# A Mamba layer on one core: the directions' B and C rows side by side in DRAM, the middle group's partitions taken in turn, the prologue's pieces spread, and the last states entering through the first token

## The chip, the cores and the metric

The kernel runs on one NeuronCore of one Trainium2 chip. The metric is the device time of one execution in microseconds, from the first to the last instruction. The kernel before takes 13002.14 us (median of three runs, 12996.56 to 13002.71); the execution that the profile shows has a span of 13002.5 us. All times below are from that profiled execution.

## The reference, cut to what matters

Two images of 96 channels and 128 x 128 pixels go through two layers. The first layer mixes with a selective scan (Mamba) in four directions and then has a quantised feed-forward part; the second mixes with a 3 x 3 convolution and has the same kind of feed-forward part. The change lies in the scan of the first layer alone. For each of the four directions, over the L = 16384 tokens of an image, with 192 inner channels d and 16 states s:

```
xc, z = split(x @ in_w.T);  u = silu(causal_conv4(xc) + conv_b)
dt_raw, B, C = split(u @ xproj_w.T)            # 6, 16, 16 columns
dt = softplus(dt_raw @ dt_w.T + dt_b);  A = -exp(A_log)
for every token t:                             # state h has 192 x 16 values
    h = exp(dt_t[:, None] * A) * h + dt_t[:, None] * B_t[None, :] * u_t[:, None]
    y_t = (h * C_t[None, :]).sum(over s)
out = ((y + Dp * u) * silu(z)) @ outp_w.T
```

B_t and C_t depend on the token and the state, not on the channel: each of their rows has to reach every partition that holds a channel.

## The kernel before, in words

The four directions are two pairs: rows with their columns forwards, and both backwards (PAIRS). The two directions of a pair have 2 x 192 = 384 channels together, that is three groups g of 128 partitions. Group 0 is all of the first direction, group 2 all of the second; the middle group 1 holds the last 64 channels of the first direction on partitions 0 to 63 and the first 64 of the second on partitions 64 to 127.

An image's scan runs over 64 *steps*: (pair, i) with 32 tiles of T = 512 tokens per pair. A step has 24 *units* (g, s): one group and two of its 16 states. The function mamba writes the instructions of all engines in a fixed order by hand (in_order), in one loop over k; I call one turn of it a *slot*, numbered 0 to 23 within a step. In the slot of unit k stand

- on ScalarE (ACT): the decays exp(dt * A) of unit k+2, two activations into a PSUM tile da (decay, L330; three such tiles), and a copy of the last token's state of unit k-1 into hst (L410);
- on GpSimd (POOL): b_part of unit k+2 (L324), which multiplies the fetched B rows by dt * u;
- on VectorE (DVE): two scans (L334) of 512 tokens, one per state, and between them the product of unit k-1's states with the C rows (L409). A scan starts from the column of hst that the step before left, or from the constant 0.0 in the first tile of a pair;
- on TensorE (PE): two identity matmuls that add unit k-1's products into one PSUM tile y per group (sums, L341). The first unit of a group opens y with the skip term (L416), and there is one such tile (ps_y has one buffer).

When a group is finished, gated (DVE, L349) multiplies y by silu(z). That happens in the slot after the next group's first unit: slots 9 (group 0), 17 (group 1) and slot 1 of the next step (group 2). Only then can the next y be opened. I use these three instants to cut a step into thirds: A from slot 1 to slot 9, B from slot 9 to slot 17, C from slot 17 to slot 1 of the next step.

In between lie the pieces that prepare the *next* step (prologue): conv and gate (PE, L207) with their evacuations conv_out and gate_out (ACT, L233, L241), two silu activations with a table load on each side (ACT, L244), the rows matmul and its evacuation rows_out (L251, L258), and for every group the softplus: dt_in (PE), dt_exp and dt_ln (three activations each), and dt_q, dt_log, dt_sum, dt_u (four tensor operations on POOL). A list of (slot, 0 or 1, piece) says where each is issued: 0 ahead of the slot's hst copy and decays, 1 behind them. The project and collect of the finished groups sit in slots 19 and 3. All PE pieces but the sums share one PSUM tile (misc, one buffer), so a conv waits until the piece before it was evacuated.

The B and C rows go through DRAM: rows_out writes four copies of 64 rows (bcd), and row_tile reads them back, four states of 512 tokens to every partition (8 KB each), 1 MB per tile. For groups 0 and 2 that is one DMA over 128 partitions, for group 1 two DMAs over 64. A tile serves two units; B tiles have four buffers, C tiles three. All DMAs are issued by SyncE (SP) in program order, and each waits there until its buffer is free.

Of the kernel before, what the change touches and what calls it, by code (L numbers as in the profile page):

```python
# [10 lines left out]
F32 = mybir.dt.float32  # L11
# [4 lines left out]
ALU = mybir.AluOpType  # L16
# [4 lines left out]
C = 96  # L21
# [11 lines left out]
COPIES = 4  # L33
# [9 lines left out]
def tile_metaformer(ctx: ExitStack, tc: tile.TileContext, a: dict, out: bass.AP):  # L43
# [35 lines left out]
    nc.vector.memset(gmat, 0.0)  # L79
    with tc.tile_pool(name="prep", bufs=1) as pp, tc.tile_pool(name="prep_ps", bufs=2, space=PSUM) as pps:  # L80
        alog = pp.tile([128, 2, NG, S], F32, name="alog")
        nc.sync.dma_start(alog, a["alog"])
        nc.scalar.activation(alog, alog, AF.Exp)
        nc.vector.tensor_scalar_mul(amat, alog, -1.0)

        dskip = pp.tile([128, 2, NG], F32, name="dskip")
        nc.sync.dma_start(dskip, a["dskip"])
        for pi in range(2):
            for g in range(NG):
                nc.vector.tensor_scalar_mul(dmat[:, pi, g, :], ident, dskip[:, pi, g : g + 1])  # L90

        inxw = pp.tile([C, 4, DI], F32, name="inxw")
        nc.sync.dma_start(inxw, a["inx"])
        taps = pp.tile([C, 4, 4, DI], F32, name="taps")
        nc.sync.dma_start(taps, a["taps"].broadcast_to((C, 4, 4, DI)))
        for d in range(4):
            nc.vector.tensor_tensor(inx[:, d], taps[:, d], inxw[:, d, None, :].broadcast_to((C, 4, DI)), ALU.mult)
        outw = pp.tile([C, 4, DI], F32, name="outw")
        nc.sync.dma_start(outw, a["outw"])
        fusew = pp.tile([C, 4, C], F32, name="fusew")  # L100
        nc.sync.dma_start(fusew, a["fusew"])
        for pi, (da, db) in enumerate(PAIRS):

            pieces = [
                (slice(0, 128), da, 0, 128),
                (slice(0, 64), da, 128, 192),
                (slice(64, 128), db, 0, 64),
                (slice(0, 128), db, 64, 192),
            ]
            for g, (rows, d, lo, hi) in enumerate(pieces):  # L110
                ps = pps.tile([128, C], F32, name="ps")
                nc.tensor.matmul(ps[rows, :], outw[:, d, lo:hi], fusew[:, d, :], start=True, stop=True)
                nc.vector.tensor_copy(gmat[rows, pi, g, :], ps[rows, :])
# [69 lines left out]
    def mamba(acc, xnr, xnc):  # L183

        with ExitStack() as st:
# [5 lines left out]
            hst = one.tile([128, NG, S], F32, name="hst")  # L191
            acc_w = acc.rearrange("c (h w) -> c w h", w=W)
# [17 lines left out]
            def prologue(pi, i, d):  # L210
# [19 lines left out]
                def conv_out(g):  # L230
                    if g == 0:
                        d["xc"] = two.tile([128, NG, T], F32, name="xc")
                    nc.scalar.activation(d["xc"][:, g, :], d["ps"], AF.Identity, bias=convb[:, pi, g : g + 1])  # L233
# [4 lines left out]
                def gate_out(g):  # L238
                    if g == 0:
                        d["sz"] = two.tile([128, NG, T], F32, name="sz")  # L240
                    nc.scalar.copy(d["sz"][:, g, :], d["ps"])  # L241
# [13 lines left out]
                def rows_out():  # L255

                    d["rows"] = one.tile([BCO + NBC, T], F32, name="rows")
                    nc.scalar.copy(d["rows"], d["ps"][0 : BCO + NBC, :])  # L258
                    d["bcd"] = rows_d.tile([COPIES, 2, NBC // 2, T], F32, name="bcd")
                    for n in range(COPIES):  # L260
                        nc.sync.dma_start(d["bcd"][n].rearrange("k r t -> (k r) t"), d["rows"][BCO:, :])
# [39 lines left out]
                at = [(0, 0, load), (8, 1, partial(silu, "xc")), (14, 1, partial(silu, "sz"))]  # L301
                at += [(12, 0, rows), (12, 1, rows_out)]
                for g, k in enumerate((4, 5, 6)):
                    at += [(k, 0, partial(conv, g)), (k, 1, partial(conv_out, g))]
                for g, k in enumerate((7, 10, 11)):
                    at += [(k, 0, partial(gate, g)), (k, 1, partial(gate_out, g))]
                for g, k in enumerate((13, 18, 21)):
                    pieces = (0, 0, dt_in), (0, 1, dt_exp), (1, 1, dt_ln), (2, 0, dt_q), (3, 0, dt_log), (3, 0, dt_sum), (4, 0, dt_u)
                    at += [(k + m, where, partial(f, g)) for m, where, f in pieces]
                return sorted(at, key=lambda p: p[:2])  # L310

            def row_tile(d, g, s, k, ahead):

                t = gen.tile([128, 4, T], F32, name=f"row{k}", bufs=ahead + 1)
                for half in range(2) if g == 1 else (slice(None),):
                    rows = slice(half * 64, half * 64 + 64) if g == 1 else half
                    at = s + S * (half if g == 1 else g // 2)
                    n = (64 if g == 1 else 128) // COPIES
                    src = d["bcd"][None, :, k, at : at + 4, :].broadcast_to((n, COPIES, 4, T))
                    nc.sync.dma_start(t[rows], src)  # L320
                return t

            def b_part(d, g, b):
                nc.gpsimd.tensor_tensor(b, d["dtu"][g][:, None, :].broadcast_to((128, 2, T)), b, ALU.mult)  # L324

# [7 lines left out]
            def scan(i, g, s, j, da, b, h):  # L333
                nc.vector.tensor_tensor_scan(  # L334
                    h[:, j, :], da[:, j, :], b[:, j, :],
                    0.0 if i == 0 else hst[:, g, s + j : s + j + 1], ALU.mult, ALU.add,
                )
# [53 lines left out]
            def feed(k):  # L391
                if k < total:
                    n = k // nu
                    b_part(state[n], units[k % nu][0], bs[k])
# [41 lines left out]
            for k in range(total + 6):  # L436
                n, u = divmod(k, nu)
                if u == 0 and n + 1 < len(steps):
                    for m, where, f in prologue(*steps[n + 1], state[n + 1]):
                        later(k + m, where, f)  # L440
                if k % 2 == 0:
                    fetch(k + 2 * B_AHEAD, 0, B_AHEAD, bs)
                feed(k + AHEAD)
                issue(k, 0)
                if k < total:
                    (_, i), (g, s) = steps[n], units[u]
                    da, b = das.pop(k), bs.pop(k)
                    hs[k] = b if (g, s) in BY_POOL else da
                    scan(i, g, s, 0, da, b, hs[k])
                if 0 < k <= total:  # L450
                    behind(k - 1)
                if k < total:
                    scan(i, g, s, 1, da, b, hs[k])
# [112 lines left out]
def _layout(v):  # L566
# [3 lines left out]
    rows = lambda w: w[order].reshape(2, NG, 128, -1).transpose(2, 0, 1, 3)  # L570
# [3 lines left out]
    for pi, pair in enumerate(PAIRS):  # L574
        for k, d in enumerate(pair):
            at = slice(k * DI, (k + 1) * DI)
            for j in range(2):
                to = slice(BCO + (2 * j + k) * S, BCO + (2 * j + k + 1) * S)
                bcw[pi, at, to] = xw[d, RK + j * S : RK + (j + 1) * S].T
            bcw[pi, at, k * RK : (k + 1) * RK] = xw[d, :RK].T  # L580
            dtw[k * RK : (k + 1) * RK, pi, at] = v["L0_conv_dt_w"][d].T
    grouped = lambda w: w.reshape(2, NG, 128, -1).transpose(2, 0, 1, 3)
# [6 lines left out]
        "convb": rows(v["L0_conv_conv_b"])[..., 0],  # L589
        "bcw": grouped(bcw),  # L590
        "dtw": dtw,
# [3 lines left out]
        "outw": v["L0_conv_outp_w"].transpose(1, 0, 2),  # L595
# [27 lines left out]
```

## Time and profile before

| engine | busy in the whole span, us | share |
|---|---|---|
| VectorE (DVE) | 11569.1 | 89% |
| TensorE (PE) matmuls | 10850.3 | 83% |
| GpSimd (POOL) | 9215.4 | 71% |
| ScalarE (ACT) | 8560.0 | 66% |
| DMA engines | mean of sixteen | 83.1% (queue 1) |

The busy share is an average. The scans of one image take about 5770 us; in their slices DVE and the DMA engines show nine tenths or more, POOL seven to eight, ACT six, PE eight. Between the two images lie some 720 us, and at the end some 570 us, of the other layers (and the normalisation ahead of the second scan), in which DVE falls to four or five tenths; the change doesn't touch them. Durations in the list of groups are from an instruction's start to its end; neighbours on one engine overlap by about 90 ns, so the distance from start to start is a little shorter than the duration.

### The profile page before, as it was taken

The numbers are of one execution on the slowest core, as the hardware profiler recorded it, in microseconds if no ns is written. First come the engines' busy times: TensorE is split into PE (matmuls) and PEld (weight loads), VectorE is DVE, ScalarE is ACT, GpSimd is POOL, SyncE is SP. The second block draws the span as 40 slices with busy tenths as digits, with TensorE's granted clock in tenths as the row PEclk, the third lists the DMA queues.
The fourth block names the chain that finished last, engine by engine and source line by source line (L and its number), as shares of the span: only waits on it lengthen the run. The fifth ranks groups of instructions, "written<-read, shape, count | busy, mean of one in ns | idle before, by whom it ended". The sixth has DMA issues, their size and how long they took to land. (4 is left out here: it accounts for less than half of the span.)

```text
span 13002.5 us, 97992 instructions
## 1 busy us (share of the span) xinstructions
PE 10850.3 (83%) x24208; PEld 3987.1 (31%) x24208; DVE 11569.1 (89%) x10865; ACT 8560.0 (66%) x14738; POOL 9215.4 (71%) x4772
## 2 busy tenths in 40 slices
PE   6888888888888888888978888888888888888889
PEld 2323233333333333333323333332333333333233
DVE  5999999999999999995459999999999999999954
ACT  6666666666666666665566666666666666666655
POOL 4877778777787787772147778777787777877721
PEclk8999999999999999999989999999999999999999
DMA  7999999999999999992079999999999999999920
GB/s 226 287 294 282 298 288 285 295 283 298 288 285 295 283 295 289 285 295 68 13 226 285 298 283 292 290 285 298 285 291 291 284 298 286 290 294 281 296 61 13
DMA packets 545331, 3400.40 MB, mean 262 GB/s; under 512 B 81612, under 2 KB 82732, under 8 KB 146840
## 3 DMA queue, kind: packets, MB, share of 16 engines
q1 hardware_dynamic: 544760, 3394.12, 83.1%
q8 instruction: 195, 3.19, 0.1%
q14 instruction: 376, 3.08, 0.1%
HBM read 3288.94 MB, written 104.86 MB: 261 GB/s over the span
## 5 line engine op out<-in xcount | busy, mean ns | idle before, releaser
L324 POOL TENSOR_TENSOR row<-dtu,row 128x1024 f32<-128x1024 f32 x3072 | 7175.7, 2358 | 1739.3 <-DMA row<-bcd 1419.2
L334 DVE TENSOR_TENSOR_SCAN da<-da,hst,row 128x512 f32<-128x512 f32 x5952 | 7339.4, 1274 | 351.2 <-ACT da L330 194.6
L341 PE MATMUL y<-row,ident 128*128 128x512 f32 x12288 | 6120.1, 626 | 1113.3 <-DVE row L409 1098.9
L330 ACT ACTIVATE da<-dt,amat 128x512 f32<-128x512 f32 x6144 | 4249.4, 692 | 207.5 <-ACT hst L410 0.4
L341 PEld LDWEIGHTS y<-row,ident 128*128 128x128 f32 x12288 | 2288.9, 197 | 4779.4 <-DVE row L409 2292.3
L409 DVE TENSOR_TENSOR row<-da,row 128x1024 f32<-128x1024 f32 x3072 | 3705.9, 1206 | 19.6 <-DMA row<-bcd 18.8
L410 ACT COPY hst<-da 128x2 f32<-128x2 f32 x3072 | 484.0, 158 | 2235.5 <-DVE row L409 2233.3
L416 PE MATMUL y<-xc,dmat 128*128 128x512 f32 x768 | 526.1, 773 | 779.1 <-DVE sz L349 779.1
L287 POOL TENSOR_TENSOR q<-e,q 128x512 f32<-128x512 f32 x384 | 488.0, 1271 | 821.8 <-ACT hst L410 709.1
L233 ACT ACTIVATE xc<-misc,convb 128x512 f32<-128x512 f32 x384 | 264.2, 688 | 1117.5 <-PE misc L207 1117.5
L207 PE MATMUL misc<-xa,inx 96*128 96x512 f32 (+1 forms) x2048 | 932.4, 597 | 59.0 <-DMA xa<-xnr 57.2
L207 PE MATMUL misc<-xb,inx 96*64 96x512 f32 (+1 forms) x2048 | 928.1, 595 | 1.6 <-ACT xc L233 1.6
L531 POOL TENSOR_TENSOR acc<-acc,y 96x512 f32<-96x512 f32 x128 | 147.6, 1153 | 987.0 <-DVE y L530 987.0
L541 PE MATMUL pc<-pad,kw 96*96 96x512 f32 x1152 | 566.7, 593 | 0.0
L207 PEld LDWEIGHTS misc<-xa,inx 96*128 96x128 f32 (+1 forms) x2048 | 323.6, 163 | 625.5 <-issue 493.4
L293 POOL TENSOR_TENSOR dt<-dt,ln 128x512 f32<-128x512 f32 x384 | 486.9, 1268 | 30.1
L297 POOL TENSOR_TENSOR dtu<-dt,xc 128x512 f32<-128x512 f32 x384 | 488.5, 1272 | 0.5
L290 POOL TENSOR_TENSOR ln<-ln,q 128x512 f32<-128x512 f32 x384 | 488.1, 1271 | 0.5
L359 PE MATMUL misc<-sz,gmat 128*96 128x512 f32 x1024 | 483.6, 594 | 0.0
L416 PEld LDWEIGHTS y<-xc,dmat 128*128 128x128 f32 x768 | 129.0, 211 | 1102.1 <-DVE sz L349 1099.1
L268 PE MATMUL misc<-rows,dtw 12*128 12x512 f32 x768 | 439.7, 652 | 18.5 <-ACT dt L275 17.2
L132 DVE TENSOR_TENSOR xq<-xm,rs 96x512 fp8e5<-96x512 f32 x128 | 87.9, 687 | 387.8 <-ACT rs L128 387.8
(75 smaller groups left out, 8403.8 us busy)
## 6 DMA issues: line engine op xcount, KB each, us to landing
row<-bcd SPq DMA_DIRECT2D x2048, 1024.0 KB, 7.5
row<-bcd SPq DMA_DIRECT2D x2048, 512.0 KB, 8.0
bcd<-rows SPq DMA_DIRECT2D x512, 128.0 KB, 9.8
xa<-xnr SPq DMA_DIRECT2D x124, 193.1 KB, 5.8
xb<-xnc SPq DMA_DIRECT2D x124, 193.1 KB, 5.5
acc<-in_x_dram SPq DMA_DIRECT2D x16, 768.0 KB, 17.8
xnr<-xn SPq DMA_DIRECT2D x16, 768.0 KB, 4.3
xnc<-stg SPq DMA_DIRECT2D x16, 768.0 KB, 5.6
```

The costliest lines, as they stand in the source:

```text
L207: nc.tensor.matmul(ps[rows, :], w(PAIRS[pi][d], k, lo, hi), src[d][:, k : k + T], **se)
L287: nc.gpsimd.tensor_tensor(d["q"], d["e"], d["q"], ALU.subtract)
L290: nc.gpsimd.tensor_tensor(d["ln"], d["ln"], d["q"], ALU.add)
L293: nc.gpsimd.tensor_tensor(d["dt"][g], d["dt"][g], d["ln"], ALU.add)
L297: nc.gpsimd.tensor_tensor(dtu, d["dt"][g], d["xc"][:, g, :], ALU.mult)
L324: nc.gpsimd.tensor_tensor(b, d["dtu"][g][:, None, :].broadcast_to((128, 2, T)), b, ALU.mult)
L330: nc.scalar.activation(da[:, j, :], d["dt"][g], AF.Exp, scale=amat[:, pi, g, s + j : s + j + 1])
L334: nc.vector.tensor_tensor_scan(h[:, j, :], da[:, j, :], b[:, j, :], 0.0 if i == 0 else hst[:, g, s + j : s + j + 1], ALU.mult, ALU.add,)
L341: nc.tensor.matmul(y, ident, c[:, j, :], start=False, stop=s + j == S - 1)
L409: nc.vector.tensor_tensor(c, h, c, ALU.mult)
L416: nc.tensor.matmul(y, dmat[:, pi, g, :], d["xc"][:, g, :], start=True, stop=False)
L541: nc.tensor.matmul(pc, kw[:, t, :], rows, start=t == 0, stop=t == 8)
```

## The change: what it does

There are four edits.

1. *One copy, ordered by use.* bcd has one copy instead of four. Its rows are ordered as [B or C][quarter of the states][direction][4 states], so that for each tile the two directions' 8 KB lie next to each other. A tile is always one DMA over 128 partitions; in group 1 even partitions read the first direction, odd ones the second.
2. *The middle group's partitions in turn.* For that the weights of group 1 are permuted on their way in (perm), so that its partitions alternate between the directions. The convolution and gate matmuls still give the old order (convb stays plain), so group 1's results go into a side tile (mix_xc, mix_sz) and two DMAs each, of 64 partitions with step 2, put them in their places. The output weights (outx) come padded, and the memset of gmat falls away.
3. *Last states through the first token.* Every scan starts from 0.0. For a tile i > 0, entering computes for each group exp(A * dt of the first token) * hst (one activation and one POOL product on 128 x 16), and b_part adds it to the first column of B (one POOL addition on 128 x 2 per unit). The copies into hst stay.
4. *Pieces spread.* The prologue's pieces move to other slots, as the list shows; group 1 comes first in conv and gate.

```
-                at = [(0, 0, load), (8, 1, partial(silu, "xc")), (14, 1, partial(silu, "sz"))]
-                at += [(12, 0, rows), (12, 1, rows_out)]
-                for g, k in enumerate((4, 5, 6)):
-                    at += [(k, 0, partial(conv, g)), (k, 1, partial(conv_out, g))]
-                for g, k in enumerate((7, 10, 11)):
-                    at += [(k, 0, partial(gate, g)), (k, 1, partial(gate_out, g))]
-                for g, k in enumerate((13, 18, 21)):
-                    pieces = (0, 0, dt_in), (0, 1, dt_exp), (1, 1, dt_ln), (2, 0, dt_q), (3, 0, dt_log), (3, 0, dt_sum), (4, 0, dt_u)
+                at = [(0, 0, load), (8, 1, partial(silu, "xc")), (13, 1, partial(silu, "sz"))]
+                at += [(12, 1, rows), (13, 0, rows_out), (13, 1, rows_to_dram)]
+                at += [(5, 0, partial(mix, "xc")), (10, 1, partial(mix, "sz"))]
+                for g, k, where in ((1, 3, 1), (0, 5, 0), (2, 6, 1)):
+                    at += [(k, where, partial(conv, g)), (k + 1, where, partial(conv_out, g))]
+                for g, k in ((1, 9), (0, 10), (2, 11)):
+                    at += [(k, 1, partial(gate, g)), (k + 1, 0, partial(gate_out, g))]
+                for g, k in enumerate((14, 17, 20)):
+                    pieces = (0, 1, dt_in), (1, 0, dt_exp), (1, 1, dt_ln), (3, 0, dt_q), (4, 0, dt_log), (4, 0, dt_sum), (5, 0, dt_u)
...
+                def mix(name):
+
+                    for k in range(2):
+                        nc.sync.dma_start(d[name][k:128:2, 1, :], d["mix", name][64 * k : 64 * k + 64, :])
...
-                    d["bcd"] = rows_d.tile([COPIES, 2, NBC // 2, T], F32, name="bcd")
-                    for n in range(COPIES):
-                        nc.sync.dma_start(d["bcd"][n].rearrange("k r t -> (k r) t"), d["rows"][BCO:, :])
+
+                def rows_to_dram():
+
+                    d["bcd"] = rows_d.tile([2, S // 4, 2, 4, T], F32, name="bcd")
+                    nc.sync.dma_start(d["bcd"].rearrange("k q d s t -> (k q d s) t"), d["rows"][BCO:, :])
...
-                for half in range(2) if g == 1 else (slice(None),):
-                    rows = slice(half * 64, half * 64 + 64) if g == 1 else half
-                    at = s + S * (half if g == 1 else g // 2)
-                    n = (64 if g == 1 else 128) // COPIES
-                    src = d["bcd"][None, :, k, at : at + 4, :].broadcast_to((n, COPIES, 4, T))
-                    nc.sync.dma_start(t[rows], src)
+
+                src = d["bcd"][k, s // 4] if g == 1 else d["bcd"][k, s // 4, g // 2 : g // 2 + 1]
+                n = src.shape[0]
+                nc.sync.dma_start(t, src[None].broadcast_to((128 // n, n, 4, T)))
                 return t
 
-            def b_part(d, g, b):
+            def entering(pi, d, g):
+
+                nc.scalar.activation(enter[:, g, :], amat[:, pi, g, :], AF.Exp, scale=d["dt"][g][:, 0:1])
+                nc.gpsimd.tensor_tensor(enter[:, g, :], enter[:, g, :], hst[:, g, :], ALU.mult)
+
+            def b_part(i, d, g, s, b):
                 nc.gpsimd.tensor_tensor(b, d["dtu"][g][:, None, :].broadcast_to((128, 2, T)), b, ALU.mult)
+                if i > 0:
+                    nc.gpsimd.tensor_tensor(b[:, :, 0], b[:, :, 0], enter[:, g, s : s + 2], ALU.add)
...
-            def scan(i, g, s, j, da, b, h):
-                nc.vector.tensor_tensor_scan(
-                    h[:, j, :], da[:, j, :], b[:, j, :],
-                    0.0 if i == 0 else hst[:, g, s + j : s + j + 1], ALU.mult, ALU.add,
-                )
+            def scan(j, da, b, h):
+                nc.vector.tensor_tensor_scan(h[:, j, :], da[:, j, :], b[:, j, :], 0.0, ALU.mult, ALU.add)
...
+                    if steps[n + 1][1] > 0:
+                        for g in range(NG):
+                            later(k + nu - 4 + nu // NG * g, 1, entering, steps[n + 1][0], state[n + 1], g)
```

## The prediction, as it was put on record

> **What bounds the kernel now.** I read the page first (busy times and slices), then the scans' line by itself, then DVE's timeline over one step, and last the busy times of that step's thirds.
>
> The page's costliest groups: line, engine, operation, operands, count, busy us, mean ns, idle time just before.
>
> ```profile
> L324 POOL TENSOR_TENSOR row<-dtu,row 128x1024 f32<-128x1024 f32 x3072 | 7175.7, 2358 | 1739.3 <-DMA row<-bcd 1419.2
> L334 DVE TENSOR_TENSOR_SCAN da<-da,hst,row 128x512 f32<-128x512 f32 x5952 | 7339.4, 1274 | 351.2 <-ACT da L330 194.6
> L409 DVE TENSOR_TENSOR row<-da,row 128x1024 f32<-128x1024 f32 x3072 | 3705.9, 1206 | 19.6 <-DMA row<-bcd 18.8
> ```
>
> Scans and products are 11 ms of DVE, with little idle time before them: DVE carries the scan part. POOL waits 1419 us for rows, but DVE's rows wait for nobody: POOL waits because it is ahead.
>
> The scans' line, min/median/max ns, the two kinds apart:
>
> ```profile
> L334 DVE TENSOR_TENSOR_SCAN da<-da,hst,row x5952: 1257/1276/1293, 253.0 to 12421.9; 128x512 f32<-128x512 f32 x199
> L334 DVE TENSOR_TENSOR_SCAN da<-da,row x192: 1201/1217/1232, 168.2 to 9630.0; 128x512 f32<-128x512 f32 x192
> ```
>
> The 192 scans of first tiles, which start from the constant, take 59 ns less, and the ranges don't touch. So the trace already holds what edit 3 makes of every scan.
>
> DVE's timeline of a step in mid-run (start, length, [idle before, releaser]):
>
> ```profile
> 1944.71 0.68 DVE L349 TENSOR_TENSOR sz<-y,sz 128x512 f32<-128x512 f32 x1
> ...
> 1973.19 0.68 DVE L349 TENSOR_TENSOR sz<-y,sz 128x512 f32<-128x512 f32 x1
> ...
> 2001.76 1.29 DVE L334 TENSOR_TENSOR_SCAN da<-da,hst,row 128x512 f32<-128x512 f32 x1 [1.75 <-ACT da L330]
> ...
> 2005.49 0.69 DVE L349 TENSOR_TENSOR sz<-y,sz 128x512 f32<-128x512 f32 x1 [1.33 <-PE y L341]
> ...
> 2033.05 1.29 DVE L334 TENSOR_TENSOR_SCAN da<-da,hst,row 128x512 f32<-128x512 f32 x1 [1.06 <-ACT hst L410]
> ```
>
> The gated products cut the step into C (1944.71 to 1973.19, 28.5 us), A (to 2005.49, 32.3 us) and B (to 2035.37, 29.9 us): 90.7 us. C has no bubble. A has one on ACT and, at its end, one on PE; B has one on ACT. A slot of C is 3.49 us, scan to scan.
>
> The same step by busy time, columns PE, PEld, DVE, ACT, POOL, granted clock, DMA share, GB/s:
>
> ```profile
> 1945.39:1973.87 28.48, 21.05 (x44) 7.44 (x44) 28.48 (x26) 19.90 (x38) 28.32 (x17) 1.00 0.89 339
> 1973.87:2006.18 32.31, 31.52 (x74) 12.27 (x74) 28.82 (x27) 16.96 (x30) 27.19 (x14) 0.95 0.84 216
> 2006.18:2036.05 29.87, 22.29 (x48) 7.56 (x48) 28.71 (x26) 23.94 (x40) 15.06 (x8) 1.00 1.01 305
> ```
>
> C is DVE's, with POOL just as full (28.32 of 28.48). A is **PE's**: 31.52 of 32.31. B is DVE's with ACT stalls. That A is PE's is proved by the step at 3050 us, whose scans all start from the constant:
>
> ```profile
> 3055.53 0.68 DVE L349 TENSOR_TENSOR sz<-y,sz 128x512 f32<-128x512 f32 x1
> ...
> 3087.82 0.69 DVE L349 TENSOR_TENSOR sz<-y,sz 128x512 f32<-128x512 f32 x1 [1.38 <-PE y L341]
> ```
>
> Its slots are 3.36 us, and its A is still 32.3: what DVE saved there went into waits. Over the whole run the thirds' means are A 31.8, B 29.9, C 28.4 us.
>
> **What the Trainium skill says.** "DMA: Bandwidth & Descriptors", Rules for kernel authors: two transfers to disjoint partition halves share the same engines, so one 128-partition transfer is better. The trace agrees: a 512 KB half takes 8.0 us to land, a whole 1024 KB tile 7.5. "GPSIMD Engine Reference", 2.1 Instruction dispatch: consecutive Pool instructions are no barrier, a reader waits for the writer's semaphore. The trace shows the price, in the first prologue's softplus:
>
> ```profile
> 151.06 1.26 POOL L290 TENSOR_TENSOR ln<-ln,q 128x512 f32<-128x512 f32 x1
> 152.40 1.27 POOL L293 TENSOR_TENSOR dt<-dt,ln 128x512 f32<-128x512 f32 x1
> ```
>
> The second needs the first and starts 0.08 us after its end; independent ones overlap by 0.05. "Perfetto Trace Analysis", Optimization Strategy: the most-contended engine can change from regime to regime. Here it does within each step.
>
> **The change, part by part.** There are 128 steps, 124 of them with hst scans.
>
> *Scans from the constant.* 48 x 0.06 = 2.9 us of DVE per step. A slot becomes 3.36 us (the step at 3050 shows it), a third without bubbles 8 x 3.36 + 0.6 (gated, start to start) = 27.5 us.
>
> *A.* PE's work decides. From the skip matmul at its start to the next one PE has: skip, 16 state sums, project, three convs, and before the change one gate (the two matmuls at L207 from inz, 0.87 us start to start). The new list moves all gates behind slot 9; the convs stay (slots 3, 5 and 6, two half a slot earlier or later). So A becomes 31.8 - 0.9 = 30.9 us, not 27.5: some 3.5 us of DVE wait stay ahead of gated. ACT's conv evacuations wait for PE as before, inside that wait.
>
> *B.* Bubbles before: 29.9 - 28.5 = 1.4 us in the mean of thirds (the one on da starts in A). The silu of sz with its two table loads (1.28 + 1.48 + 1.28 = 4.05 us) moves from slot 14 to 13 and the first softplus from 13/14 to 15. ACT's own slot work is 0.16 + 1.42 = 1.6 of 3.36 us, so 1.75 are free, and the decays are two slots ahead. Silu leaves ACT 2.3 us late, dt_exp (1.9) and dt_ln (2.0) in slot 15 take that to 2.7; written out, the decays of units 16 and 17 come 0.5 and 0.15 us late. B = 27.5 + 0.65 = 28.15.
>
> *POOL and C.* New is one addition on 128 x 2 per unit. No row shows it. POOL's time at 512 and 1024 elements (1271, 2358 ns) extrapolates to 184 ns at none; the 96 x 3 memsets take 98 ns. Bounds: 0.10 and 0.40 us (an access with a 2 KB step may cost more); I take 0.19. With the semaphore gap a unit goes from 2.31 to 2.58 us of POOL. The softplus of the first group moves from slot 15 to slot 17: all twelve of its products (1.22 each, 1.34 where one waits for the one before, 15 us) now lie in C, and group 0's can't begin before ACT ends dt_ln, some 2.7 us into C. From there to b_part of the next step's slot 1 POOL has six units (15.5), the softplus up to group 1's dt_u and one of group 2 (10.0), one entering product (0.3): 25.8 us, of which 24.8 are there. DVE waits 1.0 us, and ACT, which waits for POOL's dt_sum before the last dt_ln, adds up to 0.4. C = 27.5 + 1.2 = 28.7. The next late B rows (slots 3 and 4) fall into A, where PE is later anyway.
>
> *Costed at nothing.* Four side DMAs of 128 KB for the middle group: SP issues them behind a C tile that waits for PE, they land some 5.5 us later (xa's median 5.8), and the silus come two slots later still. Three bcd copies and one DMA per group-1 tile fewer: no DVE wait of size hangs on them. Three activations on 128 x 16 (about 0.2 us each, near the hst copy's 0.16): within ACT's free time. The gmat memset (0.7 us) against a larger outx load: hidden by the loads ahead of it. First prologues: two side DMAs in line, about 3 us each, twice for two images, together +6 to +10.
>
> *Sum.* Before 31.8 + 29.9 + 28.4 = 90.1; after 30.9 + 28.15 + 28.7 = 87.75; 2.35 us x 124 = 291, the four first steps about 2 us each, together 299, less 8 for the first prologues: 13002.5 - 291 = 12711. The profiled span stands within 0.01% of the median. I say **12,705**.
>
> **The rivals.**
>
> *POOL hides (chance 0.15).* If the addition costs 0.1 us or ACT is done a microsecond earlier, C and B are 27.5 each: 85.9 per step, 4.2 x 124 = 521 less, about 12,480. For it: POOL stood idle half of B (15.06 of 29.87). Against: it may not use that time, since its order holds dt_q ahead.
>
> *POOL becomes the bound (0.09).* At 0.4 us for the addition, C's run of six units grows by 1.3 us and slots on both sides follow: 89 per step, 12,870. The whole of POOL (24 x 2.8 + 16) would still be 83 of 89.
>
> *Slower: one copy's rows come too slowly (0.08).* All 128 partitions now read one 8 KB (or two) where four copies lay before. 24 tiles of 1.05 MB are 25.2 MB per step; as soon as they come at under 25.2 / 90.1 = 279 GB/s, DMA sets the step. The only load from a single copy, the taps at the start, ran in a stretch with 230 GB/s: that would be 109 us per step, about 15,400. Against: that stretch also moved x, with a row for each partition, no faster, and both on 96 partitions; no page of the skill bears on repeated reads of one row. A tenfold addition (from 0.6 us, POOL over 90 per step) would end there too.
>
> *No measurable change (0.02).* Every bubble taken away returns, as in the step at 3050, which gained 1.1 us of 2.9.
>
> **How the numbers follow.** The likeliest case, as summed, has 0.66, its own range 12,580 to 12,830 (1 us per step each way for ACT's and POOL's lateness). With most of the two neighbouring cases 8 in 10 lie within 12,460 to 12,910. Below 12,976 (0.2%, about what a measurement of this kernel can tell) are the first three cases, 0.89 with a little taken off the third; same 0.02; slower 0.09.
>
> **What would show it.** Right: all scans at 1217 ns; slots of 3.36; A near 31 with gated waiting for PE 3 us or more; the waits for da and hst in B under 1 us; a new wait of scans for POOL around slots 0 and 1; additions near 0.19 us; row tiles landing no later than 7.5. Wrong: DVE waiting for row DMAs, additions over 0.4 us, or A that falls to 28, which would mean that PE's order was not what held it.

## The result, and the profile after

The changed kernel takes 12841.92 us (median of four runs, 12838.81 to 12843.67) against 13002.32 us of the kernel before on the same chip: a ratio of 0.9877, 95% interval 0.986 to 0.9895. It is 160 us faster; the forecast was 12,705, so 137 us of the expected gain did not come. The profiled execution has a span of 12840.1 us.

Three groups from the page of the kernel after (scans, products with B, and the new addition):

```profile
L344 DVE TENSOR_TENSOR_SCAN da<-da,row 128x512 f32<-128x512 f32 x6144 | 7238.7, 1214 | 667.2 <-POOL row L334 401.3
L332 POOL TENSOR_TENSOR row<-dtu,row 128x1024 f32<-128x1024 f32 x3072 | 7233.3, 2355 | 38.3 <-DMA row<-bcd 31.6
L334 POOL TENSOR_TENSOR row<-row,enter 128x2 f32<-128x2 f32 x2976 | 573.7, 193 | 233.4
```

Three things have turned round. The two kinds of scan have become one, at the shorter duration. POOL's wait for fetched rows has gone from 1419 us to 32: POOL is no longer ahead of the fetches. And the scans' largest wait carries POOL's name (401 us) instead of ScalarE's. The last is what a reader would act on first, and it misleads, as the step below shows.

The scans' and the additions' lines by themselves (min/median/max ns):

```profile
L344 DVE TENSOR_TENSOR_SCAN da<-da,row x6144: 1201/1216/1232, 167.1 to 12260.4; 128x512 f32<-128x512 f32 x199
L334 POOL TENSOR_TENSOR row<-row,enter x2976: 192/193/197, 250.8 to 12248.0; 128x2 f32<-128x2 f32 x199
```

VectorE's timeline over a step in mid-run. A runs from the first gated product to the second, B to the third, C to the fourth:

```profile
1950.46 0.68 DVE L356 TENSOR_TENSOR sz<-y,sz 128x512 f32<-128x512 f32 x1
...
1957.14 1.23 DVE L344 TENSOR_TENSOR_SCAN da<-da,row 128x512 f32<-128x512 f32 x1 [1.50 <-POOL row L334]
...
1960.94 1.23 DVE L344 TENSOR_TENSOR_SCAN da<-da,row 128x512 f32<-128x512 f32 x1 [0.32 <-POOL row L334]
...
1981.51 0.69 DVE L356 TENSOR_TENSOR sz<-y,sz 128x512 f32<-128x512 f32 x1 [1.40 <-PE y L348]
...
2004.84 1.23 DVE L344 TENSOR_TENSOR_SCAN da<-da,row 128x512 f32<-128x512 f32 x1 [1.32 <-POOL row L334]
...
2010.96 0.69 DVE L356 TENSOR_TENSOR sz<-y,sz 128x512 f32<-128x512 f32 x1 [0.41 <-PE y L348]
...
2038.95 0.68 DVE L356 TENSOR_TENSOR sz<-y,sz 128x512 f32<-128x512 f32 x1
```

A has two waits for POOL (slots 3 and 4) and then the known one for PE; B has a wait at unit 16 of 1.32 us. The same step by busy time of its thirds (columns as in the prediction):

```profile
1951.14:1982.20 31.06, 29.29 (x72) 11.29 (x72) 27.84 (x26) 16.78 (x30) 30.11 (x27) 1.00 0.72 269
1982.20:2011.65 29.45, 24.45 (x50) 8.56 (x50) 27.73 (x27) 24.30 (x42) 18.89 (x17) 0.94 0.79 298
2011.65:2040.00 28.35, 21.38 (x45) 7.74 (x46) 28.06 (x26) 20.60 (x40) 26.87 (x22) 1.00 0.84 328
```

In A both PE (29.29) and POOL (30.11) are nearly full; the experiments decide which of them holds it.

**The wait whose name misleads.** These are ScalarE's entries ahead of unit 16's scan at 2004.84, and two of POOL's additions:

```profile
1996.95 0.58 ACT L260 COPY rows<-misc 96x512 f32<-96x512 f32 x1 [2.76 <-PE misc L254]
...
1999.06 1.28 ACT L247 ACT_TABLE_LOAD   x1
2000.35 1.48 ACT L247 ACTIVATE sz<-sz 128x1536 f32<-128x1536 f32 x1
2001.85 1.28 ACT L248 ACT_TABLE_LOAD   x1
...
2003.34 1.42 ACT L340 ACTIVATE da<-dt,amat 128x512 f32<-128x512 f32 x2
```

```profile
1999.45 0.19 POOL L334 TENSOR_TENSOR row<-row,enter 128x2 f32<-128x2 f32 x1
...
2004.60 0.19 POOL L334 TENSOR_TENSOR row<-row,enter 128x2 f32<-128x2 f32 x1
```

The second decay ends at 2003.34 + 1.42 = 2004.76, 80 ns before the scan. The wait is put down to POOL because an addition of POOL's ended later still, at 2004.79. But POOL does the units in order, so its operations can be counted, and the addition at 2004.60 is unit 18's. Unit 16's is the one at 1999.45: it was done at 1999.64, 3.9 us before VectorE became free for the scan (2003.52). This wait is ScalarE's alone. Matching each waiting scan with the decays and the addition of its own unit, over all steps that have additions, unit 16 waits for ScalarE's decays (161 us in 122 steps, all under POOL's name), and so do unit 20 (61 us) and unit 0 (37 us); POOL truly ends the waits of units 3 and 4 (186 and 40 us). That reading was tested, below.

### The profile page after: what moved, and what is told of

The parts are those of the page before. It is cut to its first block, busy times and chain, and to the rows that moved or that the text cites. A ratio compares the mean times of both kernels' runs of the same rounds, so it can differ in the third digit from the quotient of the medians.

```text
span 12840.1 us, 100040 instructions
## 1 busy us (share of the span) xinstructions
PE 10829.6 (84%) x24208; PEld 3988.2 (31%) x24208; DVE 11248.6 (88%) x10864; ACT 8608.7 (67%) x15110; POOL 9826.7 (77%) x8120
## 5 line engine op out<-in xcount | busy, mean ns | idle before, releaser
L344 DVE TENSOR_TENSOR_SCAN da<-da,row 128x512 f32<-128x512 f32 x6144 | 7238.7, 1214 | 667.2 <-POOL row L334 401.3
L200 PE MATMUL misc<-xa,inx 96*64 96x512 f32 (+1 forms) x2048 | 933.5, 598 | 99.1 <-ACT acc L372 40.2
L329 POOL TENSOR_TENSOR enter<-enter,hst 128x16 f32<-128x16 f32 x372 | 82.4, 221 | 1069.3 <-ACT enter L328 1069.3
L423 PE MATMUL y<-xc,dmat 128*128 128x512 f32 x768 | 473.7, 701 | 477.4 <-DVE sz L356 477.4
L334 POOL TENSOR_TENSOR row<-row,enter 128x2 f32<-128x2 f32 x2976 | 573.7, 193 | 233.4
L227 ACT ACTIVATE xc<-misc,convb 128x512 f32<-128x512 f32 x256 | 176.0, 688 | 775.4 <-PE misc L200 775.4
L277 ACT ACTIVATE e<-misc,dtb 128x512 f32<-128x512 f32 x384 | 261.1, 680 | 415.4 <-PE misc L272 404.8
L200 PEld LDWEIGHTS misc<-xa,inx 96*64 96x64 f32 (+1 forms) x2048 | 323.5, 163 | 669.8 <-issue 503.8
```

The source lines that it names most:

```text
L200: nc.tensor.matmul(ps[rows, :], w(PAIRS[pi][d], k, lo, hi), src[d][:, k : k + T], **se)
L334: nc.gpsimd.tensor_tensor(b[:, :, 0], b[:, :, 0], enter[:, g, s : s + 2], ALU.add)
L344: nc.vector.tensor_tensor_scan(h[:, j, :], da[:, j, :], b[:, j, :], 0.0, ALU.mult, ALU.add)
```

## The experiments

The kernels compare with the kernel before on the same chip; "after" stands for the changed kernel. The thirds are the mean distances between gated products over all steps, read from each trace, in us. Of the expectations printed below, those for edits 1 and 2, for edits 3 and 4 and for the last kernel of the table contain what was measured; the others missed, most of them by expecting too much, and project later by its direction.

| kernel | time, us | ratio to before | A | B | C | sum |
|---|---|---|---|---|---|---|
| before | 13002 | 1 | 31.81 | 29.85 | 28.42 | 90.08 |
| after | 12841.92 | 0.9877 | 31.13 | 29.17 | 28.54 | 88.84 |
| edits 1, 2 alone | 12998.09 | 0.9994 | 31.80 | 29.84 | 28.42 | 90.06 |
| edit 3 alone | 13067.2 | 1.0049 | 32.17 | 29.28 | 29.18 | 90.63 |
| edit 4 alone | 12908.35 | 0.9929 | 30.88 | 29.65 | 28.65 | 89.17 |
| edits 3, 4 | 12836.14 | 0.9872 | 31.14 | 29.26 | 28.52 | 88.91 |
| no additions | 12795.41 | 0.984 | 30.69 | 29.02 | 28.79 | 88.50 |
| project later | 13116.99 | 1.0089 | 31.51 | 30.25 | 29.30 | 91.06 |
| convs earlier | 12771.49 | 0.9822 | 30.10 | 29.00 | 29.24 | 88.34 |
| convs earlier, POOL 3 ahead | 12742.53 | 0.9795 | 30.18 | 28.98 | 28.80 | 87.96 |
| silu earlier | 12780.22 | 0.9823 | 31.14 | 28.72 | 28.65 | 88.51 |
| ScalarE's pieces moved | 12550.79 | 0.9652 | 31.17 | 27.70 | 27.73 | 86.60 |
| all three | 12420.66 | 0.9553 | 29.88 | 28.08 | 27.58 | 85.54 |
| all three, POOL 3 ahead | 12411.37 | 0.9544 | 29.81 | 28.09 | 27.56 | 85.46 |

### Which edit pays

**Edits 1 and 2 alone.** After, with the old list, b_part and scans (mix of xc in slot 6, of sz in slot 11, rows_to_dram in slot 12):

```
-                at += [(12, 1, rows), (13, 0, rows_out), (13, 1, rows_to_dram)]
+                at += [(12, 0, rows), (12, 1, rows_out), (12, 1, rows_to_dram)]
...
-                nc.vector.tensor_tensor_scan(h[:, j, :], da[:, j, :], b[:, j, :], 0.0, ALU.mult, ALU.add)
+                nc.vector.tensor_tensor_scan(
+                    h[:, j, :], da[:, j, :], b[:, j, :],
+                    0.0 if i == 0 else hst[:, g, s + j : s + j + 1], ALU.mult, ALU.add,
+                )
```

> Edits 1 and 2 alone on the kernel before (one copy side by side, the middle group's partitions in turn with its side tiles, mix at slots 6 and 11; old list of pieces, scans still from hst). DVE before waited for rows only 19 us in all, so faster rows have nothing to give: within 30 us of 13,002, row tiles landing in 5 us instead of 7.5 to 8, POOL's waits for rows falling from 1419 us. If one copy were a loss that the other edits hid: slower than 13,030; if rows held something: faster than 12,950.

Measured: 12998.09 us, ratio 0.9994 (0.9985 to 1.0003). The row tiles' DMA issues on its page, and POOL's wait for them in its list of waits:

```profile
row<-bcd SPq DMA_DIRECT2D x3072, 1024.0 KB, 6.9
```

```profile
POOL row L326 <- DMA row<-bcd: 912.3, 297, 7.7
```

POOL's wait for rows fell from 1419 us to 912, and the main queue's share from 83.1% to 71.7% (both from the pages), and the time did not move. All of what was saved lay in time in which POOL was ahead anyway. The rival that 128 partitions reading one 8 KB row would be slower is refuted: they land sooner (7.5 us median for a full tile before, 6.9 here), though not in the 5 us that were expected.

**Edit 3 alone.** Before, with entering, the addition and the constant start; layout and list stay:

```
+                if i > 0:
+                    nc.gpsimd.tensor_tensor(b[:, :, 0], b[:, :, 0], enter[:, g, s : s + 2], ALU.add)
...
-                    0.0 if i == 0 else hst[:, g, s + j : s + j + 1], ALU.mult, ALU.add,
+                    0.0, ALU.mult, ALU.add,
```

> Edit 3 alone on the kernel before (scans from the constant, entering and the additions; old list of pieces, four copies). If each third of a step has its own bound: A stays at 31.8 us (PE), B loses at most the 1.0 us of its eight slots, C stays near 28.5 because POOL was full there and gets some eight additions of 0.27 us: 0.3 to 0.8 us per step, 12,900 to 12,970. If DVE alone counts: 2.9 us per step, 12,640. If POOL's new work sets the time: C near 30, 13,150.

Measured: 13067.2 us, ratio 1.0049 (1.0034 to 1.0064): a loss of 65 us. Alone, the edit that shortens every scan makes the kernel slower. VectorE's waits of this kernel:

```profile
DVE da L342 <- POOL row L332: 388.4, 605, 1.6
...
DVE da L342 <- ACT da L338: 118.8, 113, 1.9
DVE da L342 <- ACT hst L415: 116.9, 103, 1.9
```

and one turn of POOL's timeline, here and in the kernel after:

```profile
2039.43 1.27 POOL L288 TENSOR_TENSOR q<-e,q 128x512 f32<-128x512 f32 x1 [4.69 <-ACT hst L415]
```

```profile
2010.00 1.27 POOL L291 TENSOR_TENSOR q<-e,q 128x512 f32<-128x512 f32 x1 [2.64 <-ACT hst L417]
```

With the old list POOL stands ahead of group 0's dt_q, idle for 4.69 us, with the B product of unit 17 as the last one done; with the new list it stands there with unit 19 done. Two units, some 5.2 us of POOL's work, are missing from its lead, and the additions use up the rest: the scans of unit 20 and of units 0 and 1 of the next step then wait for POOL (35, 83 and 38 us in all), and C becomes 29.18. A grew by 0.36 us too; that part was not taken apart.

**Edit 4 alone.** Before, with the new list and the two mix pieces left out (nothing to rearrange in the old layout):

```
-                for g, k in enumerate((4, 5, 6)):
+                for g, k, where in ((1, 3, 1), (0, 5, 0), (2, 6, 1)):
...
-                for g, k in enumerate((13, 18, 21)):
+                for g, k in enumerate((14, 17, 20)):
```

> Edit 4 alone on the kernel before (the new list of pieces without the side tiles, scans still from hst, four copies). Thirds: A loses the gate, 0.9 us; B loses its bubble of 1.4 but gets the wait for the decays of unit 16, smaller than after because slots are 3.49 us, net 0.7; C holds all twelve softplus products but no additions, no change: 1.6 us per step, about 12,800. If the list is worth little and the scans made the gain: within 30 us of 13,002.

Measured: 12908.35 us, ratio 0.9929 (0.9913 to 0.9946), 94 us faster. A is 30.88, the forecast 30.9 for just this edit's effect on it.

**Edits 3 and 4 without the layout.**

> Edits 3 and 4 on the kernel before, without the layout (four copies, two half DMAs for the middle group). Alone edit 3 cost 65 us and edit 4 gave 94, the changed kernel gives 160. If the layout gives the rest because POOL, which now has additions to do, gets its rows earlier: near the sum of the two, 12,950 to 12,980. If edits 3 and 4 gain only together and the layout is worth nothing: 12,830 to 12,860.

Its edit is the sum of the two diffs above. Measured: 12836.14 us, ratio 0.9872 (0.9857 to 0.9887), the same as the kernel after (0.986 to 0.9895). So the whole gain is that of edits 3 and 4, and they don't add up: +65 and -94 give -29 apart, -166 together. The new list gives POOL the lead that the additions need. Its row tiles take 7.4 us to land, and 8.8 for a half, where the kernel after has 5.0, and VectorE's products wait 91 us for rows there: a difference in fetching without one in time.

### What holds A

**No additions.** The activation and the product of entering stay; the additions are left out, so that no state passes from one tile to the next:

```
-                if i > 0:
+                if i < 0:
                     nc.gpsimd.tensor_tensor(b[:, :, 0], b[:, :, 0], enter[:, g, s : s + 2], ALU.add)
```

> The changed kernel without the 2976 additions to the first column (the last states do not enter; everything else as it was). Thirds: A stays at 31.1 us, since PE ends it whatever POOL does in slots 3 and 4; B stays at 29.2, since the scan of unit 16 waits for ACT's decays and not, as the profile says, for POOL; C loses 0.5 to 0.9 us, because ACT waits less for POOL's softplus: 12,730 to 12,790. If POOL's lateness is the loss, the 401 us of waits for the additions go: about 12,440.

Measured: 12795.41 us, ratio 0.984 (0.9826 to 0.9855). The additions take 574 us of POOL and cost 47 us of time, a little over a third of a microsecond per step. Without them A falls only to 30.69. Unit 3's wait for POOL falls from 186 us to 60, and unit 16's stays what it was, 161 us in 122 steps: a wait that is there without any addition is not the additions'. C grew, against the expectation: unit 20's wait rose from 61 us to 114, for a reason that comes under B and C.

**Project later.** The project of group 2 and its collect move from slot 3 to slot 9, out of A:

```
-                    later(k + 4, 0, project, pi, i, d, g)
-                    later(k + 4, 1, collect, pi, d, g)
+                    at = 4 if g == 1 or k == total - 1 else 10
+                    later(k + at, 0, project, pi, i, d, g)
+                    later(k + at, int(at == 4), collect, pi, d, g)
```

> The changed kernel with project and collect of group 2 moved from slot 3 to slot 9, both ahead of the slot's decays: 2.6 to 3.4 us of PE work leave A, nothing else changes. Thirds: A falls from 31.1 to about 29.3 us, where the waits for POOL in slots 3 and 4 (1.8) hold it; B and C as they were or 0.3 longer: 1.6 us per step, about 12,640. If A is held by POOL or DVE, no change: 12,840.

Measured: 13116.99 us, ratio 1.0089 (1.0073 to 1.0104). This one went the wrong way: 3.4 us of PE's work left A, and A became longer (31.51). PE's timeline of this kernel in an A whose gated product starts at 1902.69:

```profile
1911.76 3.36 PE L348 MATMUL y<-row,ident 128*128 128x512 f32 x4 [2.99 <-DVE row L416]
1915.05 0.91 PE L200 MATMUL misc<-xa,inx 96*64 96x512 f32 x1
```

and the first conv of the kernel after, in the A whose gated product starts at 1950.46:

```profile
1962.16 0.64 PE L200 MATMUL misc<-xa,inx 96*64 96x512 f32 x1 [0.46 <-ACT acc L372]
```

The first conv stands in slot 3 behind that slot's sums, which need slot 3's product from VectorE. With project gone PE idles 2.99 us for it, and then takes twice as long for these sums (3.36 us for four matmuls, where 1.88 to 1.98 us is usual). The conv starts 12.4 us after gated here and 11.7 us in the kernel after. From there PE runs three convs and three slots' sums without a gap. So the end of A is set by the *start* of the chain of convs and not by the amount of PE's work alone: in the kernel after, 19.35 us pass from the first conv to the next gated, early or late as it starts. The half pace has a name: the Trainium skill, "TensorE: Matmul & The Clock Gate", Part 1 (The HAM clock gate), says that the array's clock falls to half after an idle window of about 3.4 us and comes back after a busy one. The trace agrees in kind: this is the stretch after the gap by busy time, with a granted clock of 0.58; but a gap of 2.99 us was enough here.

```profile
1911.70:1915.10 3.40, 3.34 (x6) 1.01 (x6) 3.09 (x4) 1.54 (x3) 3.32 (x3) 0.58 0.57 186
```

The same trace tells the two effects apart, since not all of its steps have the long gap. Of the 122 A's that can be compared (without the first of a pair and the last of an image), 91 have a gap of about 3 us (2.67 to 3.07); in every one of them the clock falls behind it, and they last 32.0 us. In 31 the gap is 1.7 to 2.1 us, the sums behind it run at full clock, the first conv starts 11.0 us after gated, again 19.35 us pass, and A is 30.34. One of these:

```profile
1728.48 1.98 PE L348 MATMUL y<-row,ident 128*128 128x512 f32 x4 [2.10 <-DVE row L416]
```

So the move does start the chain earlier, by 0.7 us, and would shorten A by as much; the half clock after the longer gap turns that into a loss.

**Convs earlier.** After, with the first conv in slot 1 and the second in slot 4:

```
-                for g, k, where in ((1, 3, 1), (0, 5, 0), (2, 6, 1)):
+                for g, k, where in ((1, 1, 1), (0, 4, 1), (2, 6, 1)):
```

> The changed kernel with the first conv at slot 1 instead of 3 and the second at the end of slot 4 instead of ahead of 5 (the evacuations one slot later each, as before). Moving project away did not shorten A, and the convs then ran at the same times. If A is held by where the chain of three convs starts: it starts about 8 us earlier, PE's work becomes the bound again, A falls from 31.1 to 29.5, 12,640. If the lateness of POOL in slots 2 to 4 holds A: no change, 12,840.

Measured: 12771.49 us, ratio 0.9822 (0.9807 to 0.9836); A 30.10, a microsecond less, with the same work in it. PE's timeline of an A whose gated product starts at 1939.71:

```profile
1943.21 0.64 PE L200 MATMUL misc<-xa,inx 96*64 96x512 f32 x1
...
1965.80 3.60 PE L348 MATMUL y<-row,ident 128*128 128x512 f32 x8
```

PE has no idle entry from the skip matmul at 1940.44 to the last sum's end at 1969.40. Now it is the amount of work that counts: 29 us of it. C grew to 29.24, with unit 20's wait for ScalarE up from 61 us in 39 steps to 131 in 84: C took back part of what A gave.

**Convs earlier, POOL three units ahead.** In addition the B products are issued three units ahead of their scans instead of two:

```
+            for k in range(3):
+                feed(k)
             for k in range(AHEAD):
-                feed(k)
...
-                feed(k + AHEAD)
+                feed(k + 3)
```

> The kernel with the first conv at slot 1 (12,771 us), and b_part issued three units ahead instead of two, so that POOL does one more unit (2.58 us) in the 3 us for which it stands before dt_q of group 0. If POOL's lateness in slots 3 and 4 (1.8 us) is what holds A now and its softplus holds ACT in C: those waits go, A falls from 30.1 to about 29, C from 29.2 by 0.5: 12,570 to 12,640. If PE and ACT hold both: no change, 12,770.

Measured: 12742.53 us, ratio 0.9795 (0.9781 to 0.981). The waits for POOL at units 3 and 4 are gone (unit 6 waits 55 us for ScalarE), and A is 30.18 against 30.10: gated waits for PE instead (slot 9 takes 6.18 us again, 4.49 without this edit). POOL's lateness in A is hidden behind PE.

### What holds B and C

**How B's wait reaches C.** While VectorE waits at unit 16, PE gets no products. Its next entry in the step shown above, in the kernel after:

```profile
2007.24 3.68 PE L348 MATMUL y<-row,ident 128*128 128x512 f32 x4 [2.81 <-DVE row L416]
```

Four sums take 3.68 us where 1.9 is usual: from 2007.31 on the trace's clock record has PE at half for 3.41 us. This gap, or one a little longer, stands in all of 122 steps (again without the first of a pair and the last of an image), and in 120 of them the clock falls there. In 39 it stays low for two such windows or more, 6.8 us at least, and just these are the 39 steps in which unit 20 waits (1.3 to 2.0 us): its decays stand on ScalarE behind group 1's dt_exp, which waits for dt_in on PE. In the other 83 the clock is low for 3.4 us at most and unit 20 does not wait. C is 29.3 to 30.5 us long where unit 20 waits and at most 28.2 where it does not. Without the additions unit 20 waits in 81 steps and with earlier convs in 84, and this is where C grew in both. This is read from the traces; no run changed the clock alone.

**Silu earlier.** Only the silu of sz moves, from slot 13 to slot 12:

```
-                at = [(0, 0, load), (8, 1, partial(silu, "xc")), (13, 1, partial(silu, "sz"))]
+                at = [(0, 0, load), (8, 1, partial(silu, "xc")), (12, 1, partial(silu, "sz"))]
```

> The changed kernel with the silu of sz (4.05 us of ACT with its table loads) at the end of slot 12 instead of 13, so that it runs while ACT would wait for the rows matmul. If the scan of unit 16 waits for ACT's decays, as the ends of the instructions say: B falls from 29.2 to about 28.0 us, 1.2 us per step, about 12,690. If it waits for POOL's additions, as the profile names it: no change, 12,840.

Measured: 12780.22 us, ratio 0.9823 (0.9806 to 0.9839). The wait leaves unit 16, POOL's additions unchanged, and turns up at unit 15 with ScalarE (117 us); B falls from 29.17 to 28.72. A wait that moves with a ScalarE piece is ScalarE's.

**ScalarE's pieces moved.** rows_out stands behind slot 13's decays and not ahead of them, dt_exp behind its slot's decays, dt_ln ahead of the next slot's; convs and silus stay:

```
-                at += [(12, 1, rows), (13, 0, rows_out), (13, 1, rows_to_dram)]
+                at += [(12, 1, rows), (13, 1, rows_out), (14, 0, rows_to_dram)]
...
-                    pieces = (0, 1, dt_in), (1, 0, dt_exp), (1, 1, dt_ln), (3, 0, dt_q), (4, 0, dt_log), (4, 0, dt_sum), (5, 0, dt_u)
+                    pieces = (0, 1, dt_in), (1, 1, dt_exp), (2, 0, dt_ln), (3, 0, dt_q), (4, 0, dt_log), (4, 0, dt_sum), (5, 0, dt_u)
```

> The kernel after with ACT's order changed in C and B's end alone: rows_out stands behind the decays of slot 13 and rows_to_dram follows, each softplus's dt_exp stands behind the decays of its slot and its dt_ln ahead of those of the next. Convs and the silus stay where the kernel after has them. If ACT's pieces ahead of the decays are what the scans of units 16 and 20 wait for (theory), the wait of unit 16 falls from 1.3 us per step to under 0.5, those of units 20 and 0 vanish, B comes to 28.3 to 28.8 and C to 27.6, and the time to about 12,640 (12,580 to 12,720), while A stays at 31.1. If POOL sets those waits (rival: the additions and the late softplus, as the waits' names say), only the wait shifts: B stays at 29.0 or more, C at 28.4 or more, and the time within 0.3% of 12,842.

Measured: 12550.79 us, ratio 0.9652 (0.9636 to 0.9668), faster than either theory said. B is 27.70 and C 27.73, within a quarter of a microsecond of the 27.5 that a third has without bubbles; A stays at 31.17. Two thirds of this kernel by busy time (B, then C) and the scans' wait for POOL:

```profile
1929.87:1957.57 27.70, 22.75 (x50) 8.12 (x50) 27.64 (x27) 23.80 (x40) 17.87 (x16) 1.00 0.84 327
1957.57:1985.30 27.73, 21.02 (x44) 7.45 (x44) 27.70 (x27) 21.01 (x41) 27.10 (x23) 1.00 0.83 317
```

```profile
DVE da L344 <- POOL row L334: 228.8, 259, 1.6
```

VectorE is busy 27.64 of 27.70 and 27.70 of 27.73 us. The waits of units 16 and 20 are gone and unit 0's is down from 37 us to 5, with every addition in its place; of the 401 us under POOL's name 229 are left, and nearly all of them are units 3 and 4 in A. POOL has the same work in C as before and does not hold it. The mechanism at unit 16 is order: rows_out, ahead of the decays, waited 2.76 us for PE's rows matmul (1996.95 above), and all that stood on ScalarE behind it came later. Behind the decays of slot 13 it also stands behind the silu of sz, and in this trace it starts without a wait. At unit 20 two things changed at once: dt_exp stands behind the decays, and PE's gap at unit 16 with its long half clock is gone (the gaps in that stretch are 2.0 us at most). Which of the two took the wait away was not separated. The Trainium skill, "Perfetto Trace Analysis", Tensor Engine Instruction (MATMUL, LD_WEIGHTS), notes that ScalarE, VectorE and GpSimd are strictly first in, first out; this pair of kernels agrees, at 291 us for pieces that changed places with decays.

### A version that beats both

**All three** puts the earlier convs, the earlier silu and ScalarE's moved pieces together; the second kernel has POOL three ahead as well. Their edits are those shown.

> The kernel with the first conv at slot 1, the silu of sz at slot 12, rows_out behind the decays of slot 13, and each softplus with its first three activations behind the decays (the other three ahead of the next slot's hst copy), so that ACT waits for PE behind the decays and not ahead of them. If the waits at units 15, 16 and 20 are ACT's decays held up in order: B falls to about 28, C to 28: 86.2 per step, about 12,500. If they are POOL's: 12,700, the sum of the two parts alone.

> The same with b_part three units ahead. If ACT's order and POOL's lead are two separate causes: about 85 per step, 12,350 to 12,420. If POOL's lead gives nothing: as the kernel without it.

Measured: 12420.66 us (12410.62 to 12446.74), ratio 0.9553 (0.9539 to 0.9567), and 12411.37 us (12403.49 to 12415.98), ratio 0.9544 (0.9528 to 0.956): 4.5% under the kernel before and 3.3% under the kernel after; the two can't be told apart. What is left in the first, in VectorE's waits:

```profile
DVE da L344 <- POOL row L334: 229.0, 260, 1.6
...
DVE da L344 <- ACT da L340: 58.2, 99, 3.6
```

The second line is unit 15's wait, which came with the earlier silu and is why B is 28.08 here and 27.70 without it. Leaving the silu in slot 13 would by these thirds give 29.9 + 27.7 + 27.6 = 85.2 us per step, some 40 us less than 12,420; that is an estimate, and it was not run. In A the second kernel has no wait for POOL and is as long: PE's 29 us of work bound it.

## Why the prediction was right or wrong

**Right: edit 3's saving is in the trace of before.** All scans take 1216 ns, slots without a wait 3.36 us.

**Right: the addition's price.** 193 ns against 190 taken, between bounds of 0.10 and 0.40. The "tenfold addition" and the rival "POOL becomes the bound" fall with it. The entering activations take 0.29 us each, more than the 0.2 said. POOL's products with them brought its largest wait, which the prediction does not have: 1069 us for ScalarE, up to 8.5 us at a time. It takes POOL's lead from 9.8 us at unit 14 to 3.0 at unit 15 (medians), and no scan waits for it there.

**Right in size, half right in mechanism: A** (30.9 said, 31.13 measured). That PE decides A holds, since neither three units of lead for POOL (tried with the earlier convs) nor taking the additions out brings it to 27.5. But the step read PE's *work* as the bound, and the project experiment shows that in the kernel after it is where the conv chain starts. It also has no term for PE's clock: A is 31.0 where the clock stays full, and 31.4 where it falls ahead of the chain (33 of 124). The sign "gated waits for PE 3 us or more" failed: it waits 1.40 us in the step shown, because waits for POOL at units 3 and 4 stand in front and take 1.8 us of the same slack.

**Wrong in size: B, the step "ACT lateness of the decays of units 16 and 17"** (27.5 + 0.65 said, 29.17 measured). The wait was foreseen on the right engine. It reckoned 0.5 us for unit 16 and 0.15 for unit 17. Measured are slot 15 to 16 at 4.77 us, 1.41 over 3.36, and another quarter of a microsecond where gated in slot 17 waits for PE, behind the gap and the half clock shown above. Two more things were missing. A scan waits for the whole decay tile: in the step shown the two activations start at 2003.34 and end together only 1.42 us later, while the working gives one lateness for the tile and does not say whether it is the second half's. And ScalarE's own waiting for PE ahead of rows_out (2.76 us) was not in the sum of its durations. Moving rows_out and dt_exp behind the decays takes the term away entirely; how much of it each of the two made was not measured.

**Right in size, wrong in cause: C** (28.7 said, 28.54 measured). The working gave 1.0 us to scans that wait for POOL. The waits that C has, units 20 and 0 (0.50 and 0.30 us per step), end with ScalarE's decays, and go away when only ScalarE's order changes. POOL's softplus and six units fit. The smaller term, up to 0.4 us by way of ScalarE's wait for POOL's dt_sum, is borne out in kind: in the step shown ScalarE waits 0.74 and 0.71 us for POOL's softplus in front of unit 0's decays. Unit 20's wait goes with PE's half clock, which the prediction does not have, so that the size came out is luck: C is about 27.9 without that wait and 29.9 with it, and the mean lies between. The wait of units 0 and 1 for POOL that was named does exist, but in the kernel with edit 3 and the old list; in the kernel after, POOL's late rows are those of units 3 and 4.

**The sum.** A +0.23, B +1.02, C -0.16: 1.09 us per step too little, times 124 steps is 135 us, of a miss of 137. The sum as written gives 12,711; the 6 us down to 12,705 have no reason there. Measured is 12,842, inside the range given for eight in ten and 12 us above the likeliest case's own.

**The rivals.** One copy's rows too slow: refuted, by the layout alone and by a landing of 5.0 us. "POOL hides, about 12,480" did not happen to the kernel after; its reason, ScalarE being done sooner, is what the moved pieces brought (12,551, with A still at PE). Costing the layout at nothing was right: 0.9994.

## What to carry to other kernels

Price an in-order engine by when it gets to a piece, its own waits included, and not by the sum of durations: a short evacuation put ahead of work that another engine needs soon hands on its own wait. Where the profile names an engine for a wait, count that engine's operations up to the one that the waiting instruction reads: here the named addition belonged to a unit two further on, and the right one had been done 3.9 us earlier. Where an engine is full in a stretch, ask when its chain could start before taking work out of it: here starting earlier gained 1.0 us of A, and taking out 3.4 us of work opened a gap, brought the half clock and lost 0.4. And look at the single steps behind a mean before explaining it: C was about 27.9 us or about 29.9, as PE's half clock was short or long, and never the 28.5 of the table.

## What the runs showed of the hardware that was not expected

Tiny operations are not free: on POOL 193 ns for 128 x 2 and 221 ns for 128 x 16, on ScalarE 292 ns for an activation on 128 x 16 with a per-partition scale, beside 156 ns for a plain copy of 128 x 2. A row tile read from one copy lands sooner (5.0 us for 1 MB, the kernel after) than from four (7.4, the kernel with the same scans and list); these two also differ in group 1, whose tile is one DMA in the first and two in the second, so that the copy's own share is not known. PE's clock record knows two values, full and half. In the kernel after, of PE's gaps ahead of sums and skip matmuls, those of 1.4 to 1.9 us were never followed by a fall (389 gaps), those of 2.0 us in 38 of 148 cases, and those of 2.8 us in 119 of 121; the half clock then lasts 3.41 us or a multiple of it. So a rest ahead of a chain is not free, even one shorter than 3.4 us.
